# A two-layer convolution kernel on one core: where in a pair's slots its output sums, corner products and loads stand

## The chip, the core and the metric

The kernel runs on one core of a Trainium2 chip. The core has five engines that run side by side, each with its own queue of instructions that it takes in order: TensorE (PE, matrix products into PSUM), VectorE (DVE), ScalarE (ACT), GpSimd (POOL) and SyncE (SP), which here only issues transfers (DMAs). POOL issues some DMAs too. Engines wait for one another by semaphores. The metric is device time in microseconds (us), the median of several runs.

## The reference

The input is 64 images of 1024 channels with 14 x 14 pixels (float32). Two bottleneck layers follow each other; shortened:

```python
# layer 0 (batch norms over all images)
out = relu(bn(conv1x1(x, w1)))          # 1024 -> 256 channels
out = relu(bn(conv3x3(out, w2)))        # 256 -> 256
x = relu(x + softplus(residual_scale) * bn(conv1x1(out, w3)))   # 256 -> 1024

# layer 1 (group norms, each image by itself)
out = relu(group_norm(conv1x1(x, w1)))                  # 1024 -> 256
om = conv3x3(out, w_off) + b_off                        # 27 channels: offsets in x, y and a mask
sampled = bilinear_sample(out, py, px) * sigmoid(mask)  # 9 taps at shifted places
out = relu(group_norm(einsum(sampled, w2)))             # the "second conv", 256 -> 256
out = group_norm(conv1x1(out, w3))                      # the "third conv", 256 -> 1024
return relu(out + x)
```

## The kernel before

**Stages.** Layer 0 takes the first 1000 us or so: its batch norms need all images, so it runs conv by conv. Layer 1 needs one image only for a norm, and so it is pipelined over 32 pairs of images (a pair is 2 x 196 pixels in the free dimension). `slot(t)` (slots 0, 1, 30 and 31) and `steady(t)` (slots 2 to 29, 28 in all) each do, in one slot: sampling and second conv of pair t, first conv and offsets of pair t+1, third conv and output of pair t-1, and the load of pair t+2. The change touches `steady` and the two places where `slot` meets it.

**Products.** The 1 x 1 convs and the second conv are done in seven products instead of eight: weights and inputs are cut into 2 x 2 blocks, sums of the blocks are made beforehand (`first_sums` for the first conv, `first_sum` and `subtract` for the second, T for the third), and sums of the products give the outputs. `first_conv_of_seven` (L1167) has 28 products (seven m, four k): m = 1, 2, 3 need T1[1] to T1[3], the last four (m = 6) need T1[4]. After m = 3 a sum V (L1206) is made by DVE, after m = 5 and m = 6 the outputs a (L1210, L1215), then statistics (L1013) and the norm's small steps (L1023 to L1085, with one power on POOL, L1062). The scaled relu of a (L1235, ACT) is followed by `transform` (L1276 on DVE, four sums for each half of the channels, and L1280 on POOL), which the offset conv (om, L1300) reads.

**Sampling.** A pair's offsets go out to DRAM and come back spread over the partitions (wt, L1358), become distances (L1370 to L1377), go out again (wd, L1390) and come back as row factors S and column factors X (`spread_rows` L1448, `spread_columns` L1492). `corners` (L1511) multiplies S by X; three pieces for each of two sets of taps, e = 0 and e = 1. PE multiplies the transposed a (aT, L1407, L1410) with them (sp, L1531), ACT copies the result to sm (L1539), and the second conv (pd, L1643) reads sm. X of set e lies in the tile that sm of set e takes afterwards. Three PSUM banks hold sp, three more ("ps") hold the first conv, the third conv and the transposes in turn.

**Third conv and output.** For each of four j there are seven products (L1780); E is copied by ACT (L1784), V made by DVE (L1787), then two sums on POOL (L1792) and two on DVE (L1796, L1800) give z, in two tiles z0 and z1 of four channel blocks each. After the third norm ACT scales z (`scaled`, L1867), DVE adds y, the output of layer 0 (`output`, L1883, two sums of 128 x 784 for a tile), ACT does the relu (L1885) and SP stores it (L1888).

**Load.** `load(t+2, False)` reads the kept result of layer 0's last conv (h3, two DMAs of 784 KB, four channel blocks each) into y; ACT scales the eight blocks (`first_scaled`, L1103), POOL issues two DMAs that add x to y in memory (`add_x`, L1109), ACT does a relu (`first_relu`, L1118), and DVE makes the four first sums (L1130).

**Order.** In `steady`, every order is written out by hand: for PE, DVE, ACT and POOL by `manual_schedule`, for SP by `keep_in_program_order`. `at(steps, (places, extras))` puts each extra piece of work in front of the step of that number in a list of PE steps: `d1` (28 steps of the first conv of t+1), `weave(sp[0], d3[:half])` (24 steps), two steps of the third conv and the offset conv, `weave(sp[1], d3[half + 2:])` (22), `pd[0]` (35) and `pd[1]` (28). The extra's instructions stand at that place in their own engine's queue.

Of the kernel before, what the change touches and what calls it, by code (L numbers as in the profile page):

```python
# [11 lines left out]
AF = mybir.ActivationFunctionType  # L12
ALU = mybir.AluOpType
# [3 lines left out]
P = 128  # L17
H = W = 14
HW = H * W
N2 = 2 * HW  # L20
CB = 8
# [23 lines left out]
def kernel(  # L45
# [884 lines left out]
    def build_second_bottleneck(l1, path, run, early):  # L930
# [186 lines left out]
                y = Y[p % 4][:, ds(b, 2)]  # L1117
                nc.scalar.activation(y, y, AF.Relu)  # L1118

        def first_sums(p, *ns):  # L1120


            q, room = pairs[p], Z0.rearrange("p b n -> p (b n)")
            T1 = q.setdefault("T1", {})
            y = q["y"]
            (b11, b12), (b21, b22) = ([y[:, ts(c, HB), ts(i, HW)] for i in range(2)] for c in range(2))
            for n in ns:
                T1[n] = room[:, ts(n - 1, HB * HW)].rearrange("p (b q) -> p b q", b=HB)
                a, b = ((b12, b11), (b22, T1.get(1)), (b22, b12), (b21, T1.get(2)))[n - 1]
                tc.keep_in_program_order(nc.vector.tensor_tensor(T1[n], a, b, ALU.subtract))  # L1130

        def residual(p, b0=0, b1=CB):

# [33 lines left out]
        def first_conv_of_seven(p):  # L1167
            q = pairs[p]

            def step(m, k):  # L1170
                if m == k == 0:
# [10 lines left out]
                    (Se[3], T1[3]),  # L1182
                    (e12, b21),
                    (Se[4], b22),
                    (e22, T1[4]),
                )[m]
                if k == 0 and m in (0, 2, 4):
                    q["bank", m // 2] = ps.tile([P, 2, HW], FP, tag="ps", name=f"d1_{p}_{m}")
# [683 lines left out]
                        scale=n.sc[:, b, i : i + 1],  # L1872
                    )

        def output(p, m):

            q = pairs[p]
            z = q["z"][m]
            for b in range(0, HB, 2):
                part = z[:, ds(b, 2)]  # L1880

                tc.keep_in_program_order(
                    nc.vector.tensor_tensor(part, part, q["y"][:, 2 * b + m : 2 * b + m + 3 : 2], ALU.add)  # L1883
                )
                nc.scalar.activation(part, part, AF.Relu)  # L1885
            for i in range(2):
                tc.keep_in_program_order(
                    nc.sync.dma_start(  # L1888
                        out[2 * p + i].rearrange("(b m p) q -> m p b q", m=2, p=P)[m], z[:, :, ts(i, HW)]
                    )  # L1890
                )

        def finish(p, n, b):

# [56 lines left out]
        def slot(t):  # L1951
# [22 lines left out]
            weights = [lambda e=e: corners(t, e) for e in range(2)] if this else []  # L1974

            late = [lambda: scaled(t - 2, 1), lambda: output(t - 2, 1)] if t >= 2 else []

            loads = [lambda: load(t + 2)] if t + 2 < NP and not (early and t < 1) else []
            if this and not d1 and not early:
# [5 lines left out]
            if d1:  # L1985
                extra = list(zip((5, 5, 8, 12, 12, 13, 13, 14), norm2)) + [(10, w) for w in weights[:1]]
                extra = sorted(extra + [(6, s) for s in late], key=lambda v: v[0])
                todo = put(d1, [s for _, s in extra], [k * len(d1) // 16 for k, _ in extra])
# [62 lines left out]
        def steady(t):  # L2051


            sp = [sampling(t, e) for e in range(2)]
            pd = [second_conv(t, e) for e in range(2)]
            d1, d3 = first_conv(t + 1), third_conv(t - 1)
            norm1, norm2, norm3 = first_norm(t + 1), second_norm(t - 1), third_norm(t - 1, False)
            distances, end = factors(t + 1)
            half = len(d3) // 2

            def at(steps, *extra):
                extra = sorted(((k, s) for ks, l in extra for k, s in zip(ks, l)), key=lambda v: v[0])
                return put(steps, [s for _, s in extra], [k for k, _ in extra])

            todo = at(
                d1,
                ((0,), [lambda: scaled(t - 2, 1)]),
                ((2, 2, 17, 18, 18, 18, 18, 19), norm2),
                ((12,), [lambda: output(t - 2, 1)]),
                ((13,), [lambda: load(t + 2, False)]),  # L2070
                ((19, 24), [lambda n=n: corners(t, 0, n) for n in range(2)]),
            )
            todo += [lambda: corners(t, 0, 2)]
            todo += at(weave(sp[0], d3[:half]), ((4, 4, 8, 14, 16, 18, 21), norm1))
# [17 lines left out]
            todo += [lambda: list(spread_rows(t + 1, 0)), lambda: list(spread_columns(t + 1, 0))]  # L2092
            todo += [lambda: list(spread_rows(t + 1, 1)), lambda: lend(t + 1)]
            todo += at(
                pd[1],
                ((0, 22), [lambda: first_sums(t + 2, 1, 2, 3), lambda: first_sums(t + 2, 4)]),
                ((16,), [lambda: output(t - 1, 0)]),
            )
# [61 lines left out]
        def fill():  # L2160
# [33 lines left out]
            for step in steps:  # L2194
                step()

        with tc.manual_schedule(engines={mybir.EngineType.PE}):
            if early:
                fill()
            middle = range(2, NP - 2) if early else range(0)  # L2200
# [101 lines left out]
```

## Time and profile before

| what | us |
|---|---|
| median of 3 runs (lowest, highest) | 2816.66 (2815.74, 2818.49) |
| the profiled execution: its time | 2821.49 |
| its span, first to last instruction | 2819.7 |
| mean granted TensorE clock in it | 0.992 of full speed |
| one steady slot, 1294.87 to 1350.79 | 55.92 |
| busy in that slot: DVE, ACT, POOL | 49.02, 36.59, 17.77 |

The profile shows one execution. "Busy" is the time in which an engine has an instruction under way. In a timeline a row has the start, the duration, the engine, the line of the kernel, the operation, the tiles it writes and reads, and the count of instructions merged in the row; in brackets stands the idle time before it and what ended that. Some rows that the steps below use:

| row | count, mean ns |
|---|---|
| L1883 DVE, one sum of an output, 128 x 784 | 124, 967 |
| L1130 DVE, one first sum of h, 128 x 784 | 58 and 58, 971 and 970 |
| L1511 DVE, corner products of 840, 280, 672, 224 columns | 1041, 719, 848, 382 |
| L1867 ACT, one scaling of z, 128 x 196 | 496, 538 |
| L1885 ACT, one relu of an output, 128 x 784 | 124, 857 |
| L575 POOL, a sum of 128 x 784 (layer 0) | 45, 1871 and 16, 1920 |
| L1109 POOL, issue of one adding DMA; issue to landing | 56, 1921; 12.1 us |

### The profile page before, as it was taken

The numbers are of one execution on the slowest core, as the hardware profiler recorded it, in microseconds if no ns is written. First come the engines' busy times: TensorE is split into PE (matmuls) and PEld (weight loads), VectorE is DVE, ScalarE is ACT, GpSimd is POOL, SyncE is SP. The second block draws the span as 40 slices with busy tenths as digits, with TensorE's granted clock in tenths as the row PEclk, the third lists the DMA queues.
The fourth block names the chain that finished last, engine by engine and source line by source line (L and its number), as shares of the span: only waits on it lengthen the run. The fifth ranks groups of instructions, "written<-read, shape, count | busy, mean of one in ns | idle before, by whom it ended". The sixth has DMA issues, their size and how long they took to land.

```text
span 2819.7 us, 41384 instructions
## 1 busy us (share of the span) xinstructions
PE 2741.1 (97%) x13626; PEld 2108.7 (75%) x13626; DVE 2406.1 (85%) x4883; ACT 1415.2 (50%) x2806; POOL 1048.2 (37%) x1183
## 2 busy tenths in 40 slices
PE   9999899998999989999999999999999999999996
PEld 5555555554555567899889888988898889889874
DVE  7877899998788778888888888888888888888876
ACT  0000221212555545666666666666666666666653
POOL 4630366663666302323332333233323332332221
PEclk9999999999999999999999999999999999999998
DMA  7666000003656445666666656675766576757641
GB/s 230 195 172 173 26 1 0 1 1 132 220 191 225 171 136 165 156 172 193 169 163 170 191 167 165 169 201 155 169 173 195 153 175 172 201 143 175 175 133 48
DMA packets 350326, 424.33 MB, mean 150 GB/s; under 512 B 27892, under 2 KB 292500, under 8 KB 349844
## 3 DMA queue, kind: packets, MB, share of 16 engines
q1 hardware_dynamic: 291860, 376.61, 40.9%
q0 software_dynamic: 58240, 44.96, 11.4%
q8 instruction: 110, 1.80, 0.3%
q14 instruction: 116, 0.95, 0.1%
HBM read 296.49 MB, written 116.76 MB: 147 GB/s over the span
## 4 chain that ended last, share of the span: by engine, by line
PE 55%; DVE 4%; DMA 3%; issue 2%; ACT 1%; SPq 1%; POOL 0%; DVEq 0%; ACTq 0%; POOLq 0%
PE pd L1643 20%; PE sp L1531 12%; PE d L1780 10%; PE d L1190 9%; PE om L1300 2%; DMA X<-wd 1%; PE tr L1407 1%; DVE V L1787 1%; DMA wt<-dm 1%; PE pd L1562 1%; DVE sm L1599 0%; DVE st L1013 0%; ACT sm L1539 0%; DMA S<-wd 0%; SPq L1448 0%
## 5 line engine op out<-in xcount | busy, mean ns | idle before, releaser
L1531 PE MATMUL sp<-S,aT 126*128 126x420 f32 (+3 forms) x1536 | 490.7, 418 | 12.0 <-DVE S L1511 5.8
L1643 PE MATMUL pd<-sm,w2b_sb 128*128 128x196 f32 x2232 | 400.7, 329 | 0.5 <-DVE sm L1599 0.5
L1539 ACT COPY sm<-sp 128x336 f32<-128x336 f32 (+3 forms) x640 | 278.6, 452 | 220.4 <-PE sp L1531 191.3
L1643 PEld LDWEIGHTS pd<-sm,w2b_sb 128*128 128x128 f32 x2232 | 371.1, 190 | 0.9 <-DVE sm L1599 0.8
L530 PE MATMUL c<-v,u_sb 128*128 128x392 f32 x1024 | 342.9, 497 | 10.5 <-DVE bn1sh L167 8.2
L530 PEld LDWEIGHTS c<-v,u_sb 128*128 128x128 f32 x1024 | 194.6, 191 | 158.8 <-DVE v L516 11.5
L1643 PE MATMUL pd<-sm,Sc 128*128 128x196 f32 x1674 | 308.7, 329 | 1.9 <-DVE sm L1599 1.9
L1531 PEld LDWEIGHTS sp<-S,aT 126*128 126x128 f32 x1536 | 257.4, 192 | 33.0 <-ACT sm L1539 16.8
L1643 PEld LDWEIGHTS pd<-sm,Sc 128*128 128x128 f32 x1674 | 278.6, 190 | 2.7 <-ACT wt L1371 2.4
L1599 DVE TENSOR_TENSOR sm<-sm 128x980 f32<-128x980 f32 (+2 forms) x257 | 265.7, 1053 | 16.0 <-PE pd L1643 8.8
L1867 ACT ACTIVATE z<-z,gn_0sh,gn_0sc 128x196 f32<-128x196 f32 x496 | 227.7, 538 | 16.5 <-DVE gn_0sh L1085 12.5
L1674 POOL TENSOR_TENSOR E<-V,E 128x196 f32<-128x196 f32 x31 | 18.7, 603 | 519.3 <-DVE V L1673 519.3
L516 DVE TENSOR_TENSOR v<-t 128x392 f32<-128x392 f32 x256 | 192.9, 811 | 0.0
L1780 PE MATMUL d<-h,w3b_sb 128*128 128x196 f32 x744 | 174.2, 330 | 1.1 <-ACT h L1695 1.1
L1190 PE MATMUL d<-h,w1b_sb 128*128 128x196 f32 x928 | 168.2, 329 | 0.0
L1780 PEld LDWEIGHTS d<-h,w3b_sb 128*128 128x128 f32 x744 | 133.0, 189 | 44.0 <-issue 17.8
L1511 DVE TENSOR_TENSOR S<-S,X 126x840 f32<-126x840 f32 (+1 forms) x192 | 150.8, 813 | 10.7 <-DMA X<-wd 9.7
L1190 PEld LDWEIGHTS d<-h,w1b_sb 128*128 128x128 f32 x928 | 155.9, 190 | 0.2 <-DVE V L1206 0.2
L385 PE MATMUL c<-xc,w1a_sb 128*128 128x392 f32 x384 | 149.1, 497 | 5.7 <-DMA xc<-in_x_dram 5.7
L1103 ACT ACTIVATE h<-h,bn3sh,bn3sc 128x392 f32<-128x392 f32 x224 | 150.0, 706 | 0.0
L1885 ACT ACTIVATE z<-z 128x784 f32<-128x784 f32 x124 | 104.9, 857 | 77.3 <-DVE z L1883 75.1
L504 POOL TENSOR_TENSOR t<-wpad 128x784 f32<-128x784 f32 x62 | 95.3, 1538 | 125.8 <-DVE v L516 125.8
(709 smaller groups left out, 5514.5 us busy)
## 6 DMA issues: line engine op xcount, KB each, us to landing
xc<-in_x_dram SPq DMA_DIRECT2D x128, 392.0 KB
h<-o SPq DMA_DIRECT2D x64, 784.0 KB
h<-h SPq DMA_DIRECT2D x64, 784.0 KB
out_dram<-z SPq DMA_DIRECT2D x124, 392.0 KB
h<-in_x_dram POOLq DMA_DIRECT2D x56, 784.0 KB, 12.1
X<-wd SPq DMA_DIRECT2D x64, 413.4 KB
S<-wd SPq DMA_DIRECT2D x64, 413.4 KB
S<-wd SPq DMA_DIRECT2D x64, 330.8 KB
```

The source lines that it names most:

```text
L385: nc.tensor.matmul(acc[m], a, b, start=(j == 0), stop=(j == HB - 1))
L516: nc.vector.tensor_tensor(v[:, u].rearrange("p (i y x) -> p i y x", y=7, x=7), cols[c][:, :, i : i + 13 : 2, :], cols[c][:, :, j : j + 13 ...
L530: nc.tensor.matmul(m[u], u_sb[:, c, u, k % 4, ts(o, P)], vts[k][c][:, u], start=(c == 0), stop=(c == MB - 1),)
L1103: nc.scalar.activation(y, y, AF.Identity, bias=bn3.sh[:, b : b + 1], scale=bn3.sc[:, b : b + 1])
L1190: nc.tensor.matmul(bank[:, m % 2 if m < 6 else 1], a[:, k], b[:, k], start=(k == 0 and m < 6), stop=(k == HB - 1), skip_group_check=True,)
L1511: nc.vector.tensor_tensor(S[:, piece], S[:, piece], X(piece), ALU.mult)
L1531: nc.tensor.matmul(pt[:, i], q["aT"][:, i0 + i, c, starts.index(r0), :], q["corner", e][g, r0][:, :, i0 + i, :], start=(j == 0), stop=(j = ...
L1539: nc.scalar.copy(dst, pt.rearrange("p i k n -> p k i n"))
L1599: return nc.vector.tensor_tensor(dst, a, b, ALU.subtract)
L1643: nc.tensor.matmul(bank[:, m % 2], a[:, k], b[:, k - k0],  start=(k == 0 and m in (5, 0, 2, 6)), stop=(k == T - 1), skip_group_check=True,)
L1780: nc.tensor.matmul(bank[:, m % 2 if m < 6 else 1], a, b, start=(m < 6), stop=True, skip_group_check=True)
L1867: nc.scalar.activation(z[:, ts(i, HW)], z[:, ts(i, HW)], AF.Identity, bias=n.sh[:, b, i : i + 1], scale=n.sc[:, b, i : i + 1],)
```

## The change

The work is the same; its places in the steady slots differ, and one sum changes its engine.

- **Outputs.** The scalings, sums, relus and stores of both z tiles of pair t-1 stand at the end of slot t (second conv of t). Before, z1's stood in the first conv of slot t+1. `output` is cut into its sum, its relu and its store. In slot 2 (the first steady one) z1 of pair 0 is done at the start of the first conv; slot 30 has no late output any more.
- **Corner products** ("products S in front of the sums for a"): of set 0, the first stands at step 12 of the first conv, the others at step 19, so all three stand ahead of L1210. Before: steps 19 and 24, and after the first conv.
- **First sums of h**: the fourth, T1[4], is made by POOL at step 1 of the next slot's first conv (for slot 30 by DVE at step 6, in units of a sixteenth of the list); before by DVE at step 22 of the second conv's second half.
- **Load**: `load` is put at step 0 of the first conv instead of 13. Of the eight scalings L1103, two stand at step 20 of the first weave (before the last relu of a, which is at 21), three after `corners(t, 1)`, one after the offset conv, two in the second weave. `add_x` is at step 5 instead of 8; `first_relu` at 12 instead of 24 of `pd[0]`.
- **Second conv, first half**: `first_sum(t, 0)` is moved ahead into the second weave (step 9); the transposes are at 3, 5, 7, 9 instead of 6, 11, 16, 21; the end of the third norm at 11 instead of 9.

```diff
@@ first_sums
-        def first_sums(p, *ns):
+        def first_sums(p, *ns, engine=nc.vector):
...
-                tc.keep_in_program_order(nc.vector.tensor_tensor(T1[n], a, b, ALU.subtract))
+                tc.keep_in_program_order(engine.tensor_tensor(T1[n], a, b, ALU.subtract))
@@ output
+        def add_of_output(p, m, b):
...
+        def relu_of_output(p, m, b):
...
+        def store_of_output(p, m):
...
@@ slot
             late = [lambda: scaled(t - 2, 1), lambda: output(t - 2, 1)] if t >= 2 else []
+            if t - 1 in middle:
+                late = []
...
+                if early and t + 1 > middle.start + 1:
+                    extra.append((6, lambda: first_sums(t + 1, 4)))
@@ steady
+            first = [lambda: scaled(t - 2, 1), lambda: output(t - 2, 1)] if t == middle.start else []
             todo = at(
                 d1,
-                ((0,), [lambda: scaled(t - 2, 1)]),
+                ((0, 0), first),
+                ((0,), [lambda: load(t + 2, False)]),
                 ((2, 2, 17, 18, 18, 18, 18, 19), norm2),
-                ((12,), [lambda: output(t - 2, 1)]),
-                ((13,), [lambda: load(t + 2, False)]),
-                ((19, 24), [lambda n=n: corners(t, 0, n) for n in range(2)]),
+                ((1,), [lambda: first_sums(t + 1, 4, engine=nc.gpsimd)] if t > middle.start else []),
+                ((12, 19), [lambda: corners(t, 0, 0), lambda: corners(t, 0, 1, 2)]),
             )
-            todo += [lambda: corners(t, 0, 2)]
-            todo += at(weave(sp[0], d3[:half]), ((4, 4, 8, 14, 16, 18, 21), norm1))
-            todo += [lambda: corners(t, 1), lambda: first_scaled(t + 2, 0, 1, 2)]
+            todo += at(
+                weave(sp[0], d3[:half]),
+                ((4, 4, 8, 14, 16, 18, 21), norm1),
+                ((20,), [lambda: first_scaled(t + 2, 0, 1)]),
+            )
+            todo += [lambda: corners(t, 1), lambda: first_scaled(t + 2, 2, 3, 4)]
             todo += d3[half : half + 2] + offset_conv(t + 1)
-            todo += [lambda: first_scaled(t + 2, 3, 4)]
+            todo += [lambda: first_scaled(t + 2, 5)]
             todo += at(
                 weave(sp[1], d3[half + 2 :]),
                 ((4, 7), [lambda: offsets(t + 1)] + selection(t + 1)),
-                ((2, 4, 6), [lambda b=b: first_scaled(t + 2, b) for b in range(5, CB)]),
-                ((8,), [lambda: add_x(t + 2)]),
+                ((2, 4), [lambda b=b: first_scaled(t + 2, b) for b in range(6, CB)]),
+                ((5,), [lambda: add_x(t + 2)]),
+                ((9,), [lambda: first_sum(t, 0)]),
             )
             todo += at(
                 pd[0],
-                ((1, 1, 1, 9), norm3),
-                ((24, 25), [lambda: first_relu(t + 2), lambda: scaled(t - 1, 0, 4, CB)]),
-                ((5, 20), [lambda e=e: first_sum(t, e) for e in range(2)]),
-                ((6, 11, 16, 21), transposes(t + 1)),
-                ((6, 13), [distances, end]),
+                ((1, 1, 1, 11), norm3),
+                ((20,), [lambda: first_sum(t, 1)]),
+                ((3, 5, 7, 9), transposes(t + 1)),
+                ((10, 13), [distances, end]),
+                ((12, 12), [lambda: first_relu(t + 2), lambda: scaled(t - 1, 0, 4, CB)]),
+                ((14,), [lambda: scaled(t - 1, 1)]),
             )
...
+            def ends(m):
+                for b in range(0, HB, 2):
+                    relu_of_output(t - 1, m, b)
+                store_of_output(t - 1, m)
             todo += at(
                 pd[1],
-                ((0, 22), [lambda: first_sums(t + 2, 1, 2, 3), lambda: first_sums(t + 2, 4)]),
-                ((16,), [lambda: output(t - 1, 0)]),
+                ((0, 0, 4), [lambda: add_of_output(t - 1, 0, 0), lambda: first_sums(t + 2, 1, 2, 3), lambda: add_of_output(t - 1, 0, 2)]),
+                ((14, 14), [lambda b=b: add_of_output(t - 1, 1, b) for b in (0, 2)]),
+                ((16, 24), [lambda m=m: ends(m) for m in range(2)]),
             )
```

More of the change, by code (lines that the diff above doesn't have):

```diff
@@ L1184, in step @@
                     (Se[4], b22),
-                    (e22, T1[4]),
+                    (e22, T1.get(4)),
                 )[m]
@@ L1873, in scaled @@
                     )
-        def output(p, m):
+        def add_of_output(p, m, b):
             q = pairs[p]
[L1878 to L1885, printed above, removed]
+            part = q["z"][m][:, ds(b, 2)]
+            tc.keep_in_program_order(
+                nc.vector.tensor_tensor(part, part, q["y"][:, 2 * b + m : 2 * b + m + 3 : 2], ALU.add)
+            )
+        def relu_of_output(p, m, b):
+            part = pairs[p]["z"][m][:, ds(b, 2)]
+            nc.scalar.activation(part, part, AF.Relu)
+        def store_of_output(p, m):
             for i in range(2):
@@ L1888, in output @@
                     nc.sync.dma_start(
-                        out[2 * p + i].rearrange("(b m p) q -> m p b q", m=2, p=P)[m], z[:, :, ts(i, HW)]
-                    )
-                )
+                        out[2 * p + i].rearrange("(b m p) q -> m p b q", m=2, p=P)[m],
+                        pairs[p]["z"][m][:, :, ts(i, HW)],
+                    )
+                )
+        def output(p, m):
+            for b in range(0, HB, 2):
+                add_of_output(p, m, b)
+                relu_of_output(p, m, b)
+            store_of_output(p, m)
         def finish(p, n, b):
@@ L1987, in slot @@
                 extra = sorted(extra + [(6, s) for s in late], key=lambda v: v[0])
-                todo = put(d1, [s for _, s in extra], [k * len(d1) // 16 for k, _ in extra])
+                if early and t + 1 > middle.start + 1:
+                    extra.append((6, lambda: first_sums(t + 1, 4)))
+                todo = put(d1, [s for _, s in sorted(extra, key=lambda v: v[0])], [k * len(d1) // 16 for k, _ in sorted(extra, key=lambda v: v[0])])
                 todo += put(weave(sp[0], d3[:half]), norm1, (4, 4, 8, 14, 16, 18, 21))
@@ L2063, in at @@
                 return put(steps, [s for _, s in extra], [k for k, _ in extra])
+            first = [lambda: scaled(t - 2, 1), lambda: output(t - 2, 1)] if t == middle.start else []
             todo = at(
                 d1,
-                ((0,), [lambda: scaled(t - 2, 1)]),
+                ((0, 0), first),
+                ((0,), [lambda: load(t + 2, False)]),
                 ((2, 2, 17, 18, 18, 18, 18, 19), norm2),
-                ((12,), [lambda: output(t - 2, 1)]),
-                ((13,), [lambda: load(t + 2, False)]),
-                ((19, 24), [lambda n=n: corners(t, 0, n) for n in range(2)]),
-            )
-            todo += [lambda: corners(t, 0, 2)]
-            todo += at(weave(sp[0], d3[:half]), ((4, 4, 8, 14, 16, 18, 21), norm1))
-            todo += [lambda: corners(t, 1), lambda: first_scaled(t + 2, 0, 1, 2)]
+                ((1,), [lambda: first_sums(t + 1, 4, engine=nc.gpsimd)] if t > middle.start else []),
+                ((12, 19), [lambda: corners(t, 0, 0), lambda: corners(t, 0, 1, 2)]),
+            )
+            todo += at(
+                weave(sp[0], d3[:half]),
+                ((4, 4, 8, 14, 16, 18, 21), norm1),
+                ((20,), [lambda: first_scaled(t + 2, 0, 1)]),
+            )
+            todo += [lambda: corners(t, 1), lambda: first_scaled(t + 2, 2, 3, 4)]
             todo += d3[half : half + 2] + offset_conv(t + 1)
-            todo += [lambda: first_scaled(t + 2, 3, 4)]
+            todo += [lambda: first_scaled(t + 2, 5)]
             todo += at(
@@ L2093, in steady @@
             todo += [lambda: list(spread_rows(t + 1, 1)), lambda: lend(t + 1)]
+            def ends(m):
+                for b in range(0, HB, 2):
+                    relu_of_output(t - 1, m, b)
+                store_of_output(t - 1, m)
             todo += at(
                 pd[1],
-                ((0, 22), [lambda: first_sums(t + 2, 1, 2, 3), lambda: first_sums(t + 2, 4)]),
-                ((16,), [lambda: output(t - 1, 0)]),
+                ((0, 0, 4), [lambda: add_of_output(t - 1, 0, 0), lambda: first_sums(t + 2, 1, 2, 3), lambda: add_of_output(t - 1, 0, 2)]),
+                ((14, 14), [lambda b=b: add_of_output(t - 1, 1, b) for b in (0, 2)]),
+                ((16, 24), [lambda m=m: ends(m) for m in range(2)]),
             )
@@ L2195, in fill @@
                 step()
+        middle = range(2, NP - 2) if early else range(0)
         with tc.manual_schedule(engines={mybir.EngineType.PE}):
@@ L2199, in build_second_bottleneck @@
                 fill()
-            middle = range(2, NP - 2) if early else range(0)
             for t in range(0 if early else -2, middle.start):
```

## The prediction, made before the changed kernel was run

> **What bounds the kernel now.** First the busy rows of the page, then the busy times of one steady slot (from one offset convolution to the next):
>
> ```profile
> PE 2741.1 (97%) x13626; PEld 2108.7 (75%) x13626; DVE 2406.1 (85%) x4883; ACT 1415.2 (50%) x2806; POOL 1048.2 (37%) x1183
> PEclk9999999999999999999999999999999999999998
> ```
>
> ```profile
> 1294.87:1350.79 55.92, 55.58 (x347) 49.63 (x350) 49.02 (x107) 36.59 (x75) 17.77 (x23) 1.00 0.65 174
> ```
>
> TensorE (PE) is busy throughout at full clock; moving work between the others wins only what PE loses between products. PE's idle time in this slot is 0.34 us, but a busy interval also covers a product that waits, so I compared start times in PE's timeline:
>
> ```profile
> 1340.70 0.83 PE L1780 MATMUL d<-h,w3b_sb 128*128 128x196 f32 x4
> 1341.58 0.97 PE L1531 MATMUL sp<-S,aT 126*128 126x420 f32 x2
> 1342.39 0.50 PE L1780 MATMUL d<-h,Sb 128*128 128x196 f32 x2
> 1342.73 0.64 PE L1531 MATMUL sp<-S,aT 126*128 126x140 f32 x4
> 1343.62 0.57 PE L1780 MATMUL d<-T,w3b_sb 128*128 128x196 f32 x2 [0.26 <-DVE V L1787]
> ...
> 1345.17 0.87 PE L1531 MATMUL sp<-S,aT 126*128 126x420 f32 x2
> 1346.08 0.60 PE L1780 MATMUL d<-T,Sb 128*128 128x196 f32 x2
> 1346.51 0.87 PE L1531 MATMUL sp<-S,aT 126*128 126x420 f32 x2
> ```
>
> Undisturbed, two d products take 0.33 us, two sp of 420 take 0.70, four of 140 take 0.48. Here 0.88 stands for 0.67 and 0.81 for 0.70 (loss A, 0.32), 0.89 for 0.48 and 0.41 for 0.34 (loss B, 0.48), 0.91 for 0.70 and 0.43 for 0.34 (loss C, 0.30). Elsewhere only gaps of 0.06 to 0.10 remain (four, 0.34 in all). **A+B+C = 1.10 us a slot**, 28 x 1.10 = 30.8 us in the 28 steady slots: the most that can be won there. VectorE (DVE) and ScalarE (ACT) show what ends these losses:
>
> ```profile
> 1335.17 0.60 DVE L1082 SCALAR_TENSOR_TENSOR gn_5sh<-gn_5B,gn_5sc 128x4 f32<-128x4 f32 x1
> ...
> 1339.89 1.05 DVE L1511 TENSOR_TENSOR S<-S,X 126x840 f32<-126x840 f32 x1
> ...
> 1342.91 0.57 DVE L1787 TENSOR_TENSOR V<-d,E 128x392 f32<-128x392 f32 x1
> ...
> 1345.46 0.57 DVE L1796 TENSOR_TENSOR z<-d,E 128x392 f32<-128x392 f32 x1
> ...
> 1347.49 1.15 DVE L1276 TENSOR_TENSOR X<-a 128x168 f32<-128x168 f32 x4 [1.20 <-ACT a L1235]
> ...
> 1349.97 1.46 DVE L1276 TENSOR_TENSOR X<-a 128x168 f32<-128x168 f32 x4
> ```
>
> ```profile
> 1341.02 0.51 ACT L1539 COPY sm<-sp 128x420 f32<-128x420 f32 x1 [2.79 <-PE sp L1531]
> ...
> 1347.83 0.55 ACT L1235 ACTIVATE a<-a,gn_7sh,gn_7sc 128x196 f32<-128x196 f32 x1
> 1348.79 0.51 ACT L1539 COPY sm<-sp 128x420 f32<-128x420 f32 x1 [0.41 <-PE sp L1531]
> 1349.20 0.55 ACT L1235 ACTIVATE a<-a,gn_7sh,gn_7sc 128x196 f32<-128x196 f32 x1
> ```
>
> A: sm and X share a tile, so the first sm copy waits for the third corner product (DVE, to 1340.94), though its sp products began at 1337.91; three sp banks are then full and the fourth sp step waits. B: V stands behind that corner and the first norm's eight small steps. C: the bank that 1346.08 needs is freed by L1796, which waits behind the norm's scale.
>
> **The change, part by part.** Times below stay in this slot's clock (third conv starts at 1337.58). Nothing is added or removed but one engine change; the rest is order.
>
> 1. *Two output sums (2 x 0.97) leave the first conv; corners take their place.* Corner 0 (1.04) runs from 1332.74, corners 1 and 2 (0.4 + 1.0) right after the second norm's scale, done by about 1337.4 instead of 1340.94. That norm's chain keeps its root (POOL, to 1334.6), then L1078 to L1085 take 1.34 as after the root at 1344.10: 1335.95, before 1336.33. The first norm starts 1.36 earlier (1339.5), V starts 1341.55, L1796 ends 1344.6. PE without A and B wants V by 1342.9 and the bank at 1345.08. A, B and C go. DMAs: the first X has landed by 1329.1, since z's store, which by the built order waits for that X's queue semaphore, issues then; 3.6 us remain. The slower side is a later X, at a cost of what exceeds 3.6.
>
> 2. *Two of eight scalings L1103 move ahead of the last sp copies and the last relu of a.* ACT runs without a break from the sp copy at 1344.25 (two sp of 140 start 1343.57): steps of 0.41 (sm), 0.52 (relu), 0.38 (E), so relu three starts 1346.90; then 2 x 0.60 for L1103; sm 0.41; the last relu runs 1349.03 to 1349.58, before 1349.20 to 1349.75. PE now wants the second half of om at 1350.65 instead of 1351.74, so this cover is used up. What is late next is the chain behind the relu: four L1276, L1796, L1800, three L1511, offsets, L1796 of j=1, whose bank PE needs at 1358.38. It started at 1349.97, when DVE came free; now at 1349.61. Its four L1276 took 1.46, beside POOL's pair for V of j=2 (1349.20 to 1350.37); the same four took 1.15 at 1347.49. The pair will be over at 1349.5, so I take 1.15: the chain is 0.66 early, 1357.72 at its end. With 1.46 it would be 0.34. PE loses 0.10 at om, 0.09 at the next sp, 0.28 at that bank, so of 1.10 there stay **0.66 a slot, 18.5 us** (low end 0.34, 9.5 us).
>
> 3. *The h3 load behind these scalings.* They start 2.8 us earlier (1347.42; before 1350.24) and wait for the load's first half. The load issues at 1336.67; SP's order only swaps z1's store (0.96 us) ahead of X1's three loads. The shares of the DMA engines from 48 us after om on, in quarters of a microsecond, for the worst slot:
>
> ```profile
> DMA  9999999999667555555333321100000000000000
> ```
>
>    There the load ends at 1350.8 in this clock; over the slots it ends from 1346.3 to 1350.8, 1348.7 on average. The tail moves at 25 GB/s on one engine, whose share of a half (784 KB/16 = 49 KB) is 2.0 us: the first half lands 2.0 us earlier, an estimate. Then 7 slots of 27 wait 0.1 to 1.4 us, **3.9 us in all**. If both halves land together, the average wait is 1.3 us a slot; if far apart, none.
>
> 4. *Fourth sum of h on POOL.* It takes 0.97 off DVE and costs POOL the L575 row's 1.87 to 1.92 (128x784). It starts after L1675 (1329.05), ends by 1331.0; POOL's next work is the root at 1332.9 and PE's use at 1336.3. Cost nothing; without that gap the root, and all of the third conv, would be up to 1.9 late, less 1.0 of cover (0.4 that part 1 brings the relus of h2 forward, 0.6 by which the first of them ended before 1337.58). One rule speaks against it: the Trainium skill ("SBUF — State Buffer", section "Who interferes with whom") says that a DVE instruction with two SBUF inputs and a GpSimd one that reads SBUF block each other for the whole instruction. The row agrees: L1082 on four columns took 0.60 beside POOL's L1207, elsewhere 0.17. DVE's first such step of the norm is at 1331.28, after POOL is done; were it blocked throughout, up to 0.9 us a slot, 24 us, would be lost.
>
> 5. *Output sums and relus in the second conv.* DVE gains 2 x 0.97 and loses the fourth sum there. The first sum of sm0 (1.17) goes into the 1.04 idle at 1303.1, so the rest stands 1.2 earlier. add_x follows 1.3 earlier and POOL's 3.2 us for it clear sooner. I get DVE free at 1326.5, before V at 1327.2; ACT's relus end 1328.4, before E at 1331.15. Cost nothing; if the cover goes, 0.7 us must be exceeded first. z1's store moves 3 us forward; its tile is next written at 1355.6.
>
> 6. *Edges.* Slot 2 does the old scalings and sums in a row before the second norm (about 0.4 us, once), slot 30 loses its late outputs and gains one sum. The stall of 1.31 at 2660.28 may go. I set the edges to zero, bounds -3 to +3 us.
>
> **Sum.** -18.5 + 3.9 = -14.6. The profiled execution had a span of 2819.7 and 1.8 around it, 2821.5; it becomes 2806.9. It stood 4.8 above the median of the runs, 2816.66; I take the 14.6 us off the median: **2802 us**.
>
> **Rivals.**
> - *DVE's chain keeps the slot* (22%). The four L1276 stay at 1.46 or more and the load waits cost some: 0 to 0.35 a slot, 2807 to 2817, typically -5 us, 2812. For it: PE in before lost only 0.06 at that bank, so DVE and PE are already even there. Against: POOL's pair does move away.
> - *The scalings wait for the load* (22%, the slower side). If the first half lands with the second, or the load's tail grows as all stores come earlier, ACT stands at the moved L1103 and with it the relu, the offsets and PE at om. Break-even is a landing 0.66 after 1347.42; at the average 1348.7 the wait of 1.3 leaves 1.3 - 0.66 = +0.6 a slot, +18 us: 2835. Against: the waiting instruction names the first half alone.
> - *PE's floor* (8%): nothing given back, -1.10 x 28 = -31, 2786.
> - *It does not do what it says*: the new order is on all engines as described, so only the size is open: 2816.7 if the losses have other causes; its chance lies in the first rival's.
>
> **How the numbers follow.** Forecast 48%, with its own range 2793 to 2810. 0.2% (5.6 us, about what a measurement can tell from no change) puts the borders at 2811 and 2822. Faster: 48 + 8 + a quarter of the chain case (5) = 61%. Same: the rest of the chain case and a small part of the load case, 19%. Slower: 20%. The range 2791 to 2828 cuts most of the floor and the upper two thirds of the load case, some 20%.
>
> **What would show it.** Slots of 55.2 to 55.4 us (before 55.9). No idle of PE at V L1787; the first sm copy right behind its sp products (1338.8); L1276's second group 1.2 us long. Wrong if ACT L1103 waits for DMA h in most slots, if PE waits at om for DVE, or if L1034 beside the POOL sum grows from 0.22.

## The result, and the profile after

The changed kernel takes **2882.83 us** (median of 4 runs, 2874.80 to 2886.31) against 2816.36 for the kernel before on the same chip: a ratio of 1.0231, 95% interval [1.0208, 1.0254]. It is 66 us slower; the forecast was 14.6 us faster (2802, range 2791 to 2828). The profiled execution has a span of 2884.5 us at a mean clock of 0.988.

The page after: busy time, share and instructions by engine, and the chain of waits that ended last; below it the same chain of the kernel before.

```profile
PE 2752.7 (95%) x13626; PEld 2121.9 (74%) x13626; DVE 2370.1 (82%) x4856; ACT 1410.1 (49%) x2806; POOL 1088.4 (38%) x1210
...
DMA 22%; DVE 15%; PE 13%; ACT 6%; issue 4%; POOL 2%; SPq 2%; DVEq 0%; ACTq 0%; POOLq 0%
```

```profile
PE 55%; DVE 4%; DMA 3%; issue 2%; ACT 1%; SPq 1%; POOL 0%; DVEq 0%; ACTq 0%; POOLq 0%
```

PE has the same instructions and 2 points less share, and the chain that ends last now runs through transfers (DMA 22% instead of 3). PE's timeline in a steady slot shows two things at once:

```profile
1347.28 0.83 PE L1780 MATMUL d<-h,w3b_sb 128*128 128x196 f32 x4
1347.94 0.87 PE L1531 MATMUL sp<-S,aT 126*128 126x420 f32 x2
1348.65 0.50 PE L1780 MATMUL d<-h,Sb 128*128 128x196 f32 x2
1348.98 0.64 PE L1531 MATMUL sp<-S,aT 126*128 126x140 f32 x4
1349.46 0.50 PE L1780 MATMUL d<-T,w3b_sb 128*128 128x196 f32 x2
...
1350.94 0.87 PE L1531 MATMUL sp<-S,aT 126*128 126x420 f32 x2
1351.64 0.50 PE L1780 MATMUL d<-T,Sb 128*128 128x196 f32 x2
...
1356.19 1.16 PE L1300 MATMUL om<-X,woff_sb 128*32 128x196 f32 x24
1360.80 2.15 PE L1300 MATMUL om<-X,woff_sb 128*32 128x196 f32 x24 [3.45 <-DVE X L1276]
```

First, the losses are gone as forecast: the steps of 0.33 and 0.48 ahead of the V product (B stood there with 0.89) are the undisturbed ones, and the same holds at A and C (1347.28 to 1347.94, 1350.94 to 1351.64). Second, the offset conv stops between its halves for 3.45 us, and waits for DVE's L1276.

The second half also takes 2.15, where all 48 products of the kernel before took 2.10. Two things lengthen it. In most of the 26 slots between 1177 and 2700 us it takes 1.4 us instead of 1.06 up to the next row: its first products start while DVE's four sums L1276 are still under way. And in the slot shown the granted clock of PE falls. Of three stretches, here are the length, the busy times of PE, PEld, DVE, ACT and POOL, and then the granted clock (1.00, 0.50, 1.00), the DMA engines' share and GB/s:

```profile
1356.19:1357.35 1.16, 1.15 (x25) 0.67 (x24) 0.00 (x0) 0.00 (x0) 0.00 (x0) 1.00 0.58 225
1361.45:1364.86 3.41, 3.41 (x26) 2.24 (x15) 2.91 (x7) 2.01 (x5) 0.00 (x0) 0.50 0.00 0
1365.00:1370.00 5.00, 5.00 (x30) 4.40 (x29) 4.42 (x13) 4.29 (x10) 3.72 (x4) 1.00 0.08 12
```

It falls to 0.50 in seven of the 26 slots, each time near PE's restart after such a stop (of 2.0 to 4.2 us), for 3.4 us and once for 6.8, but not after every stop of that length. From these lengths I estimate up to 13 us of the loss. In the kernel before, the clock is full throughout the same stretch.

The waits between 1177 and 2700 us (total, times, longest) lead back to the load:

```profile
ACT h L1103 <- DMA h<-h: 68.6, 26, 4.6
...
PE om L1300 <- DVE X L1276: 58.2, 26, 4.2
```

and ACT's timeline shows one of the 26, with the moved scalings waiting for the load:

```profile
1298.69 1.32 ACT L1103 ACTIVATE h<-h,bn3sh,bn3sc 128x392 f32<-128x392 f32 x2 [3.26 <-DMA h<-h]
```

The last relu of a stands behind these two scalings in ACT's queue (1300.30), L1276 behind the relu (1300.88), the second half of om behind L1276. So the rival "the scalings wait for the load" came true, in all 26 slots and with a mean wait twice as long (2.6 us instead of 1.3). SP's timeline tells why the load is late. Before (third conv at 1337.58) and after (third conv at 1344.15):

```profile
1329.09 2.58 SPq L1888 DMA_DIRECT2D out_dram<-z  x2
1331.83 3.61 SPq L1492 DMA_DIRECT2D X<-wd  x3
1335.55 0.96 SPq L1888 DMA_DIRECT2D out_dram<-z  x2
1336.67 2.41 SPq L204 DMA_DIRECT2D h<-h  x2
```

```profile
1336.76 6.32 SPq L1890 DMA_DIRECT2D out_dram<-z  x4
1343.24 2.39 SPq L1492 DMA_DIRECT2D X<-wd  x3
1345.81 0.82 SPq L204 DMA_DIRECT2D h<-h  x2
```

The four stores in a row hold SP's queue for 6.3 us (median of the slots), where the two pairs took 4.0 together. Relative to the third conv, the start of the load's issue moves from -0.55 to +1.09 us (medians over the slots). The landings stand in the trace too, as the last semaphore update of each half: the first half lands 9.6 us after the third conv's start in the kernel before and 12.3 in the changed one (10.2 and 11.2 after its issue), and the second 1.9 us later in both. The moved scalings are ready at 9.7. The issue alone does not explain these 2.7 us: in the kernel before SP stands 1.6 us in issuing the first half, in the changed one 0.35, so its end moves only from +1.08 to +1.43. The three loads of X1, which stand right ahead of the load in the changed order, start 3.7 us later than before (-1.7 instead of -5.4); whether they hold the load back was not tested.

### The profile page after: what moved, and what is told of

It is laid out like the page before. It is cut to its first block, busy times and chain, and to the rows that moved or that the text cites. A ratio compares the mean times of both kernels' runs of the same rounds, so it can differ in the third digit from the quotient of the medians.

```text
span 2884.5 us, 41169 instructions
## 1 busy us (share of the span) xinstructions
PE 2752.7 (95%) x13626; PEld 2121.9 (74%) x13626; DVE 2370.1 (82%) x4856; ACT 1410.1 (49%) x2806; POOL 1088.4 (38%) x1210
## 4 chain that ended last, share of the span: by engine, by line
DMA 22%; DVE 15%; PE 13%; ACT 6%; issue 4%; POOL 2%; SPq 2%; DVEq 0%; ACTq 0%; POOLq 0%
DMA h<-h 11%; DMA wt<-dm 7%; PE pd L1643 5%; PE sp L1531 3%; PE d L1780 3%; DVE st L1013 2%; DVE sm L1599 2%; ACT h L1118 2%; PE om L1300 2%; DMA X<-wd 2%; ACT h L1103 1%; ACT z L1867 1%; DVE h L1130 1%; DVE z L1880 1%; DMA aT<-aT 1%
## 5 line engine op out<-in xcount | busy, mean ns | idle before, releaser
L1674 POOL TENSOR_TENSOR E<-V,E 128x196 f32<-128x196 f32 x31 | 18.6, 602 | 528.5 <-DVE V L1673 528.5
L1103 ACT ACTIVATE h<-h,bn3sh,bn3sc 128x392 f32<-128x392 f32 x224 | 150.6, 709 | 71.3 <-DMA h<-h 71.3
L1276 DVE TENSOR_TENSOR X<-a 128x168 f32<-128x168 f32 x248 | 72.0, 354 | 127.6 <-ACT a L1235 127.6
L1792 POOL TENSOR_TENSOR E<-V,E 128x196 f32<-128x196 f32 x124 | 74.1, 598 | 194.1 <-DVE V L1787 167.9
L1511 DVE TENSOR_TENSOR S<-S,X 126x840 f32<-126x840 f32 (+1 forms) x192 | 139.8, 767 | 9.0 <-DMA X<-wd 9.0
```

What stands on the lines that cost most here:

```text
L1103: nc.scalar.activation(y, y, AF.Identity, bias=bn3.sh[:, b : b + 1], scale=bn3.sc[:, b : b + 1])
L1511: nc.vector.tensor_tensor(S[:, piece], S[:, piece], X(piece), ALU.mult)
```

## The experiments

Every run is one kernel, its median, and its ratio to the kernel before on the same chip (medians 2819.4 to 2821.2) with the 95% interval. "Slot" is the distance of two offset convs; waits are sums between 1177 and 2700 us. e16 to e18 leave out the addition of x in the steady slots, so they compute less.

| run | edit | us | ratio |
|---|---|---|---|
| e1 | changed, scalings and x back | 2783.39 | 0.9871 [0.9855, 0.9888] |
| e2 | changed, z1's store behind X1 | 2824.61 | 1.0016 [1.0006, 1.0026] |
| e3 | before, scalings and x early | 2867.43 | one run |
| e4 | before, corners early | 2825.32 | 1.0019 [1.0009, 1.0029] |
| e5 | e1, fourth sum on DVE | 2792.19 | 0.9904 [0.9888, 0.9921] |
| e6 | changed, x held | 2869.57 | 1.0186 [1.0167, 1.0205] |
| e7 | e6 and e2 together | 2819.79 | 1.0004 [0.9995, 1.0014] |
| e8 | before, scalings early but the last | 2865.64 | 1.0164 [1.0147, 1.0181] |
| e9 | changed, load ahead of the stores | 2852.55 | 1.0103 [1.0077, 1.0128] |
| e10 | before, scalings early, x late | 2879.79 | 1.0215 [1.0198, 1.0232] |
| e11 | e9 and x late | 2881.64 | 1.0219 [1.0197, 1.0242] |
| e12 | e1, load ahead of the stores | 2827.09 | 1.0015 [0.9997, 1.0033] |
| e13 | changed, only the last scalings and x early | 2789.99 | 0.9901 [0.9883, 0.9920] |
| e14 | e3, distances at 10 | 2860.34 | 1.0140 [1.0123, 1.0157] |
| e15 | e1, corners back | 2797.73 | 0.9924 [0.9907, 0.9940] |
| e16 | e3 without x | 2819.92 | 1.0001 [0.9991, 1.0011] |
| e17 | before without x | 2811.75 | 0.9969 [0.9956, 0.9981] |
| e18 | changed without x | 2832.77 | 1.0049 [1.0030, 1.0069] |

The theory after the result: the moved scalings wait for the load, and that is the whole loss. The rival: moving them (and `add_x`) costs by itself.

### The scalings back (e1), the store later (e2), the scalings alone (e3)

```diff
 e1, the changed kernel:
-                ((20,), [lambda: first_scaled(t + 2, 0, 1)]),
-            todo += [lambda: corners(t, 1), lambda: first_scaled(t + 2, 2, 3, 4)]
+            todo += [lambda: corners(t, 1), lambda: first_scaled(t + 2, 0, 1, 2)]
-            todo += [lambda: first_scaled(t + 2, 5)]
+            todo += [lambda: first_scaled(t + 2, 3, 4)]
-                ((2, 4), [lambda b=b: first_scaled(t + 2, b) for b in range(6, CB)]),
-                ((5,), [lambda: add_x(t + 2)]),
+                ((2, 4, 6), [lambda b=b: first_scaled(t + 2, b) for b in range(5, CB)]),
+                ((8,), [lambda: add_x(t + 2)]),
 e2, the changed kernel:
-                store_of_output(t - 1, m)
+                if m == 0:
+                    store_of_output(t - 1, m)
+            todo.append(lambda: store_of_output(t - 1, 1))   # behind spread_columns(t + 1, 1)
 e3: the lines of e1 the other way round, in the kernel before
```

> The changed kernel with the eight scalings L1103 and add_x at the places they had before; all else as changed. Theory W (the whole loss is ScalarE standing at the two scalings that were moved ahead of the last relu of a, until the h3 load lands: 26 waits, 68.6 us): without them the rest of the change gains what the prediction summed, 0.5 to 0.7 us a slot, so 2798 to 2806 us, slots of 55.2 to 55.4. Rival D (the corners, the sum on GpSimd or the packed second conv cost as well): 2817 us or more. Rival L (the load lands so late that the scalings wait at their old places too): 2820 to 2850, with waits of ACT L1103 for DMA h in most slots.

e1 gives 2783.39: 3.5% below the changed kernel (0.9871/1.0231), 1.3% below the kernel before, and less than the theory expected. PE has no idle time worth naming in a steady slot (2.1 us of waits in 1523 us); most slots take 54.74 to 54.76. So all that the change loses hangs on the place of the scalings and of `add_x`, about 100 us.

> The changed kernel with one edit: the store of z1 is issued after the three X1 loads, as before, instead of ahead of them. Theory Q (the load lands late because SP issues it 2.6 us later behind z1's stores): SP issues the load within 0.5 us of the place it had before (0.9 us ahead of the third conv), the wait of 2.6 us a slot falls under 1 us, 2805 to 2830 us. Rival B (the landing is set by what the DMA engines still have to move, not by the order of issue): wait and time as in the changed kernel, 2870 to 2890 us.

The load is issued at -0.10 again and its first half lands at 10.3, and 58 us of the 100 come back. L1103 still waits 21.4 us in all, 23 times: with the order of SP as before, the load is still too late for the new place. e1 shows the other side: with the changed order and x at its old place the first half lands at 11.6. So of the 2.7 us that it is late in the changed kernel, about 2.0 go with the order of the stores and 0.7 with what moved x (9.6, 11.6, 12.3; 9.6, 10.3).

> The kernel before with the scalings L1103 and add_x alone at their new places. It shows when the first half of the load lands in the order before. By the prediction's estimate (2.0 us ahead of the end of the tail) ACT waits in 7 slots of 27, 4 us in all, and the time is 2815 to 2825 us. If the halves land nearly together, or as long after their issue as in the changed kernel (12 us), ACT waits 1 to 2 us in nearly every slot, PE waits at om for DVE, and the time is 2835 to 2865 us.

e3 was a surprise. Its scalings waited for the load once (0.6 us), and yet 2867 instead of 2820. (They were ready only at 10.9, so e3 does not test where they would meet the load in the changed kernel.) What it shows instead is DVE waiting at L1370 for the broadcast of the offsets (wt, 37.6 us and 11.9 more at that line) and PE at pd for DVE's sums (28.5 us):

```profile
DVE wt L1370 <- DMA wt<-dm: 37.6, 20, 2.6
...
PE pd L1643 <- DVE sm L1599: 28.5, 26, 1.8
```

In the kernel before POOL's `add_x` was held by the last scaling. With the scalings early it starts sooner: SP's issue of wt stands 2.22 us behind x's instead of 1.14 (medians). That became a second theory: x's transfer gets in front of wt's.

### Is it x's transfer? (e6, e7, e8, e10, e14)

```diff
 e6, the changed kernel (e8: the same in e3; e7: with e2's line too):
-                ((2, 4), [lambda b=b: first_scaled(t + 2, b) for b in range(6, CB)]),
-                ((5,), [lambda: add_x(t + 2)]),
+                ((2, 6), [lambda b=b: first_scaled(t + 2, b) for b in range(6, CB)]),
+                ((8,), [lambda: add_x(t + 2)]),
 e10, e3 with:
-                ((5,), [lambda: add_x(t + 2)]),
+            todo += [lambda: add_x(t + 2)]       # behind the second weave, ahead of pd[0]
 e14, e3 with:
-                ((6, 13), [distances, end]),
+                ((10, 13), [distances, end]),
```

> The changed kernel, with the scaling of the last block of h3 back at step 6 of the second half of the third convolution and the addition of x at 8, as before; the other scalings stay early. GpSimd's transfer of x is held by that last scaling, so it starts about 1 us later against the offsets' transfers than in the changed kernel. Theory 'two waits': the early transfer of x gets in front of the broadcast of wt on the DMA engines and costs what the changed kernel with z1's store late still lost against the one with the scalings back, 2825 - 2783 = 41 us; the wait of the scalings for the load of h3 stays. So 2883 - 41 = 2842, with wt L1370 waiting for its DMA under 10 us in all and L1103 waiting near 69 us. Rival 'one wait': the wait at wt only follows from the late load, so nothing changes, 2883.

> As the one before, and z1's store behind the loads of X1, which lets SP issue the load of h3 as early as in the kernel before. Theory 'two waits': 2825 - 41 = 2784, plus what the remaining waits of L1103 (21 us in all with the store late, of which 13 reached PE) cost: 2784 to 2797. Rival 'one wait': the transfer of x is not to blame, 2825 as with z1's store late alone.

> The kernel before with the scalings of h3 early, except that of the last block, which stays at step 6 with the addition of x at 8. Compared with the kernel before in which all of them and the addition of x were early (2867) it differs by the place of one scaling of 0.7 us and so by about 1 us in the start of x's transfer. Theory 'the transfer of x in front of wt': the whole loss goes, 2820 (1.000, within 8 us), and wt L1370 waits for its DMA under 10 us in all. Rival 'early scalings delay ACT's other work': 2867 or near it, with wt's wait as it was (35 us).

The theory missed in all three: e6 won 13 us instead of 41, e7 5, e8 next to nothing (2 us, against a single run). e7 and e8 came out near what their rivals said. The hold was too weak to decide: in e8 wt was issued 1.70 us behind x, not 1.14, and wt's wait stayed (37.3 us). So e10 put x behind wt altogether.

> The kernel before with all scalings of h3 early, and the addition of x behind GpSimd's last copies of the third convolution, about 4 us later than in the kernel before, so that the broadcasts of wt are on the DMA engines first. Theory 'x in front of wt': wt L1370 waits under 10 us in all for its DMA and the whole loss of the early scalings (2867 against 2820) goes: 2820, unless the relus of h3 now wait for x on ACT. Rival 'the early scalings delay the offsets themselves': wt's wait of 35 us stays, and the time is 2860 or more.

```profile
DVE h L1130 <- ACT h L1118: 97.0, 52, 4.2
...
ACT h L1118 <- DMA h<-in_x_dram: 62.8, 26, 3.4
```

DVE no longer waits for wt at all, so x's transfer was what made wt late. But now x lands too late for the relu of h, and DVE's first sums stand behind that: 2880. x has a narrow place, with a loss on either side.

> The kernel before with all scalings and the addition of x early (2867), and with the distances, DVE's first instruction that needs wt, at step 10 of the second convolution's first half, where the changed kernel has them, instead of at 6. Theory 'the late wt costs by the place at which DVE waits for it': DVE sums sm first, PE's wait at pd (27 us) goes, and 2867 falls to 2820-2830. Rival 'DVE is late by the same amount wherever it waits': 2860 or more.

7 us, and PE's wait at pd stays (22.4 us): the wait only moves on (DVE L1377 now waits 37.5 us for ACT's L1372). The rival was right here.

### The load first (e9, e11, e12)

```diff
-                ((0,), [lambda: load(t + 2, False)]),
+                ((0,), [lambda: load(t + 2, False)] if t == middle.start else []),
+                ((15,), [lambda: load(t + 3, False)] if t + 1 < middle.stop else []),   # in pd[1]
```

> The changed kernel with one thing moved: the load of h3 is issued on SP ahead of the four stores of a slot instead of behind them and X1's loads (in the slot before, behind the last sum that reads its buffer). Scalings and addition of x stay early. Theory 'the load is the whole loss': L1103 waits for its DMA under 10 us in all, and the slots go to 55.1, the shortest that the kernel with z1's store late had, against 54.76 with the scalings back: 2783 + 28 x 0.35 = 2793. Rival 'the early transfer of x in front of wt costs most of the rest': L1103 no longer waits, yet the time stays at 2815 to 2825, with wt L1370 waiting for its DMA about 40 us.

> The changed kernel with the scalings back, and the load of h3 ahead of the stores. Theory 'SP's order costs nothing as long as nobody waits': 2783, as with the scalings back alone (ratio 0.987). Rival 'X1's loads, another 2 us later, reach the second products late': PE waits at sp for DVE's S, 0.3 us or more in a slot, 2792 or more.

> The changed kernel with both: the load of h3 ahead of the stores, and the addition of x behind GpSimd's last copies of the third convolution. If the load and the place of x's transfer are the two causes, nothing of the loss is left: slots of 54.8, 2783 to 2788. Rival 'x comes too late for the relus': ACT L1118 waits for in_x in most slots and the sums of h on DVE with it, 2795 or more.

The theories of all three missed. In none does a scaling wait for the load in most slots, and each has a new wait; e12, where PE had hardly waited, loses 44 us:

```profile
DVE z L1796 <- DMA out_dram<-z: 54.7, 25, 3.1
```

The stores now go out behind the load, and DVE's first write of the next z waits until the tile has been read. So the load can't simply be put first: on SP's queue three kinds of transfers each have a latest place (the stores for the next z, X1 for the products S, the load for the scalings). e11 adds e10's late x, and its rival came true: L1118 waits 89.3 us for it, 26 times.

### How much is the load, how much x (e13, e16, e17, e18)

```diff
 e13, the changed kernel:
-                ((20,), [lambda: first_scaled(t + 2, 0, 1)]),
-            todo += [lambda: corners(t, 1), lambda: first_scaled(t + 2, 2, 3, 4)]
+            todo += [lambda: corners(t, 1), lambda: first_scaled(t + 2, 0, 1, 2)]
-            todo += [lambda: first_scaled(t + 2, 5)]
+            todo += [lambda: first_scaled(t + 2, 3, 4, 5)]
 e16 (in e3), e18 (in the changed kernel); e17 in the kernel before, at 8:
-                ((5,), [lambda: add_x(t + 2)]),
+                ((5,), []),
```

> The changed kernel with the first scalings of h3 back (blocks 0, 1, 2 behind the corners), and only the last ones and the addition of x early: block 5 ahead of the second sampling products, 6 and 7 at 2 and 4, x at 5. So nothing waits for the load (as with all scalings back), while the transfer of x still starts about 1 us early. Theory 'the wait for the load is most of the 100 us between the changed kernel and the one with the scalings back': 2783 to 2792 (ratio 0.987 to 0.990). Rival 'x in front of wt costs the rest that z1's late store left': 2815 or more, with wt L1370 waiting about 40 us for its DMA and PE at pd for DVE's sums.

2790: with only the first scalings back, 93 of the 100 us are gone, though DVE still waits for wt:

```profile
DVE wt L1370 <- DMA wt<-dm: 26.4, 16, 2.9
...
ACT h L1103 <- DMA h<-h: 11.6, 13, 1.2
```

PE's waits at pd are 1.4 us in all here, so wt's wait on DVE is covered. Note that x is held a little by the later scalings (wt is issued 1.41 us behind it, not 2.22).

> Leaves out the addition of x in the steady slots (the two transfers on GpSimd's queue), so it computes less: the kernel before with all scalings of h3 early (2867 with the addition). Compared with the next kernel, which leaves the same out with the scalings in their old places. Theory 'the early scalings cost 45 us in the kernel before only through x's transfer': the two are equal within 6 us, and wt L1370 doesn't wait for its DMA. Rival 'they also cost on ACT, whatever x does': this one is 20 us or more slower than the next.

> Leaves out the addition of x in the steady slots, so it computes less: the kernel before otherwise. The control of the kernel ahead of it. PE's losses A, B and C don't hang on x, so 2815 to 2820 if x was hidden in the kernel before; lower by what GpSimd's 3.2 us a slot for issuing and DVE's three waits at wt (2 us in all) cost, at most 10 us.

The early scalings cost 8.2 us without x (2819.92 - 2811.75), between the two expectations, against 48 with it (e3; 46 in e8). So about 40 of e3's 48 us come through the addition of x. POOL's 3.2 us of issuing it are left out as well here; that the transfer is the part that counts rests on the waits at wt, which are gone in e16 and in e10.

> Leaves out the addition of x in the steady slots, so it computes less: the changed kernel otherwise. Theory 'the wait for the load is some 93 of the 100 us, x's early transfer some 7': 2870 to 2878 instead of 2883, L1103 waiting for its DMA about 69 us in all as before. Rival 'the load is late because x's transfer holds the queues': the wait at L1103 falls below 40 us, and the time below 2850.

This went the rival's way: L1103's wait falls from 68.6 to 37.4 us and the time by 50 us (8 of which leaving x out also saved in the kernel before). Without x, SP's first store is issued 1.87 us earlier against the third conv (-9.86 instead of -7.99, medians) and the load with it (-0.77 instead of +1.09): S, aT, the stores and the load stand behind wt's chain in SP's queue, so what delays wt delays the load. The two causes meet in one chain. That 58 us (the stores in a row, e2) and about 42 (x, e18) sum to 100 is not a proof that they add: both kernels still wait for the load, 21.4 and 37.4 us. So the wait for the load is most of the loss (e13), and the early x is one of two reasons why the load is late.

### What wins the 1.2 us a slot (e4, e5, e15)

```diff
 e4, the kernel before:
-                ((19, 24), [lambda n=n: corners(t, 0, n) for n in range(2)]),
-            todo += [lambda: corners(t, 0, 2)]
+                ((19, 19), [lambda: corners(t, 0, 0), lambda: corners(t, 0, 1, 2)]),
 e15, e1 with the corners' old places (the - lines of e4)
 e5, e1 with T1[4] on DVE at step 22 of pd[1]
```

> The kernel before with one part of the change alone: all three corners of product 0 of the third convolution are issued at step 19 of the first convolution instead of at 19, 24 and after it. The prediction booked stall A, 0.32 us in a slot, to the late third corner. Theory 'each stall is its own': A goes and 0.3 us x 28 = 9 us are saved, 2811 against 2820 (0.997). Rival 'DVE's chain sets the slot, so a stall removed ahead of it comes back at the next wait': B grows by what A loses, 2820 (1.000). A trace without idle PE ahead of the sp banks and with an unchanged wait at V L1787 is for the first; a longer wait at V is for the second.

```profile
1286.41 0.64 PE L1531 MATMUL sp<-S,aT 126*128 126x140 f32 x4
1287.80 0.57 PE L1780 MATMUL d<-T,w3b_sb 128*128 128x196 f32 x2 [0.75 <-DVE V L1787]
```

A is gone and B has grown from 0.26 to 0.75: the rival, and a little worse. Here the stall that was removed comes back at PE's next wait for DVE, whose work ahead of V is the same.

> The changed kernel with the scalings back (2783), and the three corners of product 0 back at 19, 24 and after the first convolution as in the kernel before; the output sums stay packed. With the corners alone early in the kernel before, the time rose by 0.2%: stall A went, B grew from 0.26 to 0.75 us. Theory 'the room that the moved sums leave on DVE is what wins, and the corners need it': stall A comes back, 0.3 x 28 = 9 us, 2792. Rival 'the corners' place no longer matters with that room': 2783.

With the output sums out of the way, the corners' place is worth 14 us (slots 55.27 against 54.76), more than A alone.

> As e1 (scalings back), and the fourth sum of h on VectorE at step 22 of the second half of the second conv, as before. If the sum on GpSimd costs nothing, as predicted, this is the same or up to 0.3 us a slot slower than e1 (VectorE then reaches V of the second conv 0.3 us late): e1 to e1 + 9 us. If GpSimd blocks VectorE for the sum's 1.85 us, this is faster than e1 by 10 us or more.

The sum on POOL is worth 8.8 us.

## Why the prediction was wrong

- **What bounds the kernel: right.** A + B + C = 1.10 us a slot were real and removable: e1's slot is 1.16 below 55.92.
- **Part 1, corners for output sums: right.** A, B and C go. The corners alone win nothing (e4); without them 14 of e1's 36 us are missing (e15).
- **Part 2, the give-back: wrong.** It held that PE would lose 0.44 a slot behind the relu of a, with the scalings moved to limit that. The moved scalings brought the four L1276 to 1.19, as forecast; but in e1, with the scalings in their old places and L1276 at 1.42, PE loses nothing there. (The text's three losses, 0.10, 0.09 and 0.28, sum to 0.47, not to the 0.44 that its 0.66 leaves.) The cover that it called used up was not needed, and the forecast of the "floor" rival, 2786, is what e1 shows (2783).
- **Part 3, the load behind the scalings: the step that failed.** It summed the waits to 3.9 us by leaving the load's landing where it was: "SP's order only swaps z1's store (0.96 us) ahead of X1's three loads". The place in the old order was estimated well: the halves land 1.9 us apart (2.0 in the text), the first 9.6 us after the third conv's start (9.1 in the text, 1346.7). But the change moved it to 12.3. The load's issue starts 1.6 us later against the third conv, with four stores in a row that hold SP for 6.3 us instead of 4.0 and a chain from wt on that is late; and from there it takes 11.2 us instead of 10.2. So the mean wait is 2.6 us a slot, against 0.14 in the sum. Two of the prediction's own signs of being wrong, L1103 waiting for h in most slots and PE waiting at om, came true. The mechanism and even its victim (the relu, the offsets, PE at om) stood in the rival; its price of 2835 took 1.3 us for the wait and set 0.66 against it.
- **Part 4, the fourth sum on POOL: right, and better.** POOL took 1.85 us (1335.64), and DVE's steps beside it kept their times (L1677 0.57, L1013 0.57 and 0.58, L1683 0.34). The Trainium skill's rule on DVE and GpSimd blocking each other ("SBUF — State Buffer", section "Who interferes with whom") was not put to the test, since none of those steps reads two inputs in SBUF; the first that did, L1034 at 1337.91, came after the sum and took 0.23. (The row cited for the rule, L1082 with 0.60 beside POOL and 0.17 elsewhere, has a third value: 0.52 at 1344.72, beside POOL's L1792.) The text priced the freed 0.97 us of DVE at nothing; e5 shows 8.8 us.
- **Part 5: right on the sums, wrong on a clause.** PE no longer waits for V. But "add_x follows 1.3 earlier" was costed at nothing. The earlier transfer made wt late, and through wt's chain the load. The profile of before had the warning: `add_x` is held by the last scaling in all 27 of its slots (27.2 us of POOL's idle time), which kept x 1.14 us ahead of wt's issue and no more. The text named POOL's time for it, and not the DMA engines that its packets share with SP's.
- **Part 6:** e1's gain of 36 us is 28 x 1.16 = 32.5 and some 4 at the edges, about the bound given.

**What stays open.** In the kernel before, wt's delay by x is shown (e10, e16), and that about 40 us come through its addition; why the early x costs that much there and almost nothing in e13 is only argued: DVE has more room ahead of the sums of sm in the changed order, and x was somewhat less early. The load's lateness splits into about 2.0 us from the order of the stores and 0.7 from x; how the 100 us split is open, and so is why the transfers ahead of the load end later than the shift of its issue.

## What to carry to other kernels

When an instruction is moved ahead, look up when its data land, from the issue on: which queue issues the load, everything that the change puts ahead of it in that queue, and the measured time from issue to landing. A transfer that starts earlier competes with what it used to follow; before an edit loosens the wait that held it, find who is next on the same DMA engines. And try the parts apart: here one part of a losing change was worth 1.3%, and the losing part was not needed by it.

## What was not expected of the hardware

- x's transfer (POOL's queue) makes wt's (SP's) late though no semaphore joins them. With wt issued 1.1 us behind x, DVE's first use hardly waited for it (2.2 us in all in the kernel before, 4.1 in e1); at 1.4 us behind, 26 us (e13); at 1.7 to 2.2 us behind, about 30 to 40 us (2.8 in e14, where that use stands later); with x behind wt, not at all (e10). The Trainium skill ("DMA: Bandwidth & Descriptors", section "Issuing engines are not separate DMA queues") says that transfers from different engines run on the same 16 DMA engines and interleave; these rows agree.
- An issue on SP takes longer the earlier x's transfer starts: that of mk (L1358) took 0.79 us in the kernel before, 1.27 in e13 and 1.51 in the changed kernel, and 0.79 with x behind it or left out (e10, e18; medians).
- A stop that the profile books as idle is only a part of it. In e2, PE idled 13.0 us at om, and the om products' own busy time grew by another 13.7 us against e1 (65.7 to 79.4).
- Around a stop of PE of 2 us or more the granted clock can fall to 0.50 for 3.4 us. In the changed kernel that happened seven times, in e6 nine times, and in e9, e11 and e12 ten times, there behind stops at d. In e3, e8 and e10, whose waits of PE are at most 1.8 us long, it did not happen between 1177 and 2700 us.
